# A six-layer network on one core: the experts' transposes a pair further ahead, the zero rows behind the second sample's norm, and a fixed order for the feed-forward's sums

## The chip, the cores and the metric

The kernel runs on one core of one Trainium2 chip. The metric is device time in microseconds (us) of one launch, which computes the whole network for a batch of eight samples. A core has five engines, each with an instruction stream of its own that is executed in order: TensorE (PE in the profile; its weight loads are shown as PEld), VectorE (DVE), ScalarE (ACT), GpSimd (POOL) and SyncE (SP). SyncE issues nearly all transfers; it is written SPq where the profile speaks of its queue. An instruction that waits for a signal of another engine holds everything behind it on its own engine.

## The reference

The input is x of shape (8, 256, 32, 32). Six layers follow one another: an attention with convolutions and a gated convolutional feed-forward, a deformable convolution, a causal attention, a feed-forward on half of the tokens, an attention with squared scores, and a mixture of eight experts. The change touches the last three, where a sample is 1024 tokens of 256 numbers. Cut to these:

```
def _L2_ffn_ref(x, attention_mask, wr, br, w1, b1, w2, b2):
    weights = (jnp.einsum('bsd,do->bso', x, wr) + br)[..., 0]
    _, idx = jax.lax.top_k(weights, k)                 # k = 512 of 1024 tokens
    sel_idx = idx[:, :kk]                              # kk = 511
    sel = jnp.take_along_axis(x, sel_idx[:, :, None], axis=1)
    h = jax.nn.gelu(jnp.einsum('bkd,dh->bkh', sel, w1) + b1)     # 256 -> 1024
    y = jnp.einsum('bkh,hd->bkd', h, w2) + b2                    # 1024 -> 256
    y = y * jnp.take_along_axis(weights, sel_idx, axis=1)[..., None]
    return jnp.zeros_like(x).at[batch_idx, sel_idx].set(y) + x

def _L3_attn_ref(x, qkv_w, qkv_b, proj_w, proj_b):     # 8 heads of 32
    scores = jnp.einsum('bnhd,bmhd->bhnm', q, k) * scale
    t = jnp.square(scores + 5.0)
    attn = t / jnp.sum(t, axis=-1, keepdims=True)
    return jnp.einsum('bhnm,bmhd->bnhd', attn, v).reshape(B, N, D) @ proj_w.T + proj_b

def _moe(tokens, router_w, w1, b1, w2, b2):            # 8 experts, 2 of them for a token
    probs = jax.nn.softmax(tokens @ router_w.T, axis=-1)
    rw, re = jax.lax.top_k(probs, 2)
    rw = rw / jnp.maximum(rw.sum(-1, keepdims=True), 1e-12)
    out = tokens
    for e in range(E):
        h = jax.nn.gelu(tokens @ w1[e] + b1[e], approximate=False)
        out = out + combine[:, e:e + 1] * (h @ w2[e] + b2[e])
    return out
```

Each of these layers is called as `t = t + layer(_ln_t(t))`, with `_ln_t` the normalisation of a token.

## The kernel before

**How work is ordered.** Each layer is a Python generator (`fast0` to `fast3e`) that writes instructions and yields between pieces. A layer's first pieces ("head") are drawn while the layer before it still runs. Inside a layer, `spread` (L1067) lays one generator's pieces evenly beside another's, and `by_time` (L1093) merges several by due times. What the generators write is then put in a final order on each engine by a scheduler; an instruction handed to `net.pinned` (L1042) keeps its written place among the other pinned ones of its engine. `scatter` (L1023) is an indirect transfer from POOL that writes rows to places given by an index; `settled` (L1034) makes a load wait for all the scatters of a group.

**Feed-forward (`fast2f`, about 2640 to 2935 us).** For each sample, `before(b)` norms the tokens and computes a token's score as eight sums on VectorE (L2116, one for each 128 tokens, into a column of `wcol`), then adds the bias `br` (L2119, "wcol"). TensorE transposes `wcol` (L2124, "wrow"), ScalarE copies the rows, and comparisons give each token its rank. `place(b)` scatters tokens in that order to memory, `ready(b)` loads the best 512, transposes them on TensorE (L2178, "xs") and copies them out on VectorE (L2183, "xk"). `main(b)` does the two products: h, gelu, and y with sums over 1024 (L2200); VectorE adds the bias b2 to y in two halves (L2207, "y add"). The streams of several samples are interleaved, so that the scores of one sample lie beside the y products of another on VectorE. Neither L2119 nor L2207 is pinned.

**Attention (`fast3`, about 2935 to 3950 us).** Sample b's attention has 33 steps (`attention`), each with four products s of keys and queries, two squares on ScalarE and four products A with the values; at the end of a chunk VectorE scales the sum (L2660, "o"), and adds the projection (L2666). Beside sample b's steps, `between(b)` is spread: the routing of sample b - 1 (`Routes.route`: norm, store of the normed rows at L2376 "mox", scores of the eight experts, ranks), and the norm and projections of sample b + 1 (`norm`, `projections`). `norm` loads the sample at L2555, writes the normed tokens (`token_norm_steps`, L1019) to a tile `xt`, whose buffer the router's `mo_x` shares, and transposes them on TensorE (L2564, "xn"). For b = 0 there is no sample to route, and `between(0)` begins with `Routes.fill` (L2345): one tile of zeros (a memset at L2350, three small sums at L2352) is stored eight times by SP (L2359, "so<-zero"), to fill the three sorted lists of tokens with rows that no token will take.

**Experts (`fast3e`, about 3950 to 4370 us).** The samples are in three groups (0 to 2, 3 to 5, 6 and 7). `Routes.sort(g)` scatters each group's tokens twice, once for each chosen expert, in the order of experts, into its sorted list in memory ("so"), a token's destination beside it. `experts` then goes over the 76 pairs of blocks of 128 sorted rows, two blocks each but for the last of a group with an odd number. For a pair q:

- `load(q)` loads the rows into `xs` (L2779), one of five buffers, four pairs ahead (`AHEAD`).
- `weights(q)` copies the first product's weights of the blocks' experts on ScalarE (L2792).
- `fetch(q)` transposes the rows on TensorE (L2807, "a") and copies them out on VectorE (L2809, "xk", two buffers).
- `first(q)` does the first product (L2821, "h", sixteen for a pair) and four gelus on ScalarE (L2827, "hid").
- `second(q)` casts the destinations to integers on POOL (L2839, "to"), does the second product (L2843, "y"), adds the bias on VectorE (L2847) and scatters the result (L1026).

`combine(g)` adds up the results of a finished group while the next group runs: loads yg, VectorE sums (L2909, "s"), transposes (L2920, "oT") and stores. The rows of the last group are sorted beside the first groups' pairs; `sorting` is the number of steps over which this is spread. The loop of `experts` is, in the kernel before:

```
            weights(0)
            fetch(0)
            yield
            for q in range(len(pairs)):
                weights(q + 1)
                first(q)
                yield
                fetch(q + 1)
                if q:
                    second(q - 1)
                yield
            second(len(pairs) - 1)
```

Of the kernel before, what the change touches and what calls it, by code (L numbers as in the profile page):

```python
# [10 lines left out]
F32 = mybir.dt.float32  # L11
# [6 lines left out]
P = 128  # L18
B = 8
C = 256  # L20
# [2023 lines left out]
def fast2f(net, io):  # L2044
# [5 lines left out]
    with ExitStack() as ctx, ExitStack() as mid:  # L2050
# [26 lines left out]
        def before(b):  # L2077
# [37 lines left out]
            for t in range(NT):  # L2115
                nc.vector.scalar_tensor_tensor(  # L2116
                    junk[:, :C], xn[:, t, :], 1.0, wr, ALU.mult, ALU.mult, accum_out=wcol[:, t : t + 1]
                )
            nc.vector.tensor_scalar(wcol, wcol, vec[:, 10:11], None, ALU.add)  # L2119
            yield  # L2120
            yield from scaled(s, 2)
            ps = pair("wrow")
# [63 lines left out]
        def main(b):  # L2186
            xk = xks.pop(b)
            hid = own["two"].tile([P, H // P, S], F32, tag="hid", name="hid")
            for m in range(H // P):
                ps = bank("h")  # L2190
                net.linear(ps, w1, xk, bass.ts(m, P), slice(0, S))
                net.pinned(nc.scalar.activation(hid[:, m, :], ps, AF.Gelu_apprx_tanh, bias=vec[:, m : m + 1]))
                yield
            y = own["two"].tile([P, 4, C], F32, tag="y", name="y")
            pk = picked[b] = dr.tile([S, C], F32, tag=f"pk{b}", name=f"pk{b}")
            for t2 in range(0, 4, 2):
                ps = bank("y")
                for i in range(2):
                    for k in range(H // P):
                        made = nc.tensor.matmul(  # L2200
                            ps[:, bass.ts(i, C)], lhsT=hid[:, k, bass.ts(t2 + i, P)], rhs=w2[:, k, :],
                            start=(k == 0), stop=(k == H // P - 1),
                        )
                        if k == 0:
                            net.pinned(made)
                    yield
                nc.vector.tensor_tensor(  # L2207
                    y[:, t2 : t2 + 2], ps.rearrange("p (t c) -> p t c", c=C),
                    b2.unsqueeze(1).to_broadcast([P, 2, C]), ALU.add,
                )  # L2210
            nc.sync.dma_start(out=pk.rearrange("(t p) c -> p t c", p=P), in_=y)
            yield
# [83 lines left out]
class Routes:  # L2296
# [49 lines left out]
    def fill(self):  # L2346

        nc = self.net.nc
        zero = self.rows_of.tile([P, len(GROUPS), ROW], F32, tag="xl", name="zero")
        nc.vector.memset(zero, 0.0)  # L2350
        for g, (lo, hi) in enumerate(GROUPS):
            nc.vector.tensor_scalar(  # L2352
                zero[:, g, C:], self.dest[:, 0:1].to_broadcast([P, ROW - C]), float((hi - lo) * 2 * N), None, ALU.add
            )
        for g, so in enumerate(self.sorteds):
            self.fills[g] = []
            for lo in range(0, TILES[g], 26):
                hi = min(TILES[g], lo + 26)
                ins = nc.sync.dma_start(  # L2359
                    out=so[lo * P : hi * P].rearrange("(t p) c -> p t c", p=P),  # L2360
                    in_=zero[:, g : g + 1].to_broadcast([P, hi - lo, ROW]),
                )
                self.fills[g].append(ins.ins)
                yield

# [140 lines left out]
def fast3(net, io):  # L2506
# [4 lines left out]
    with ExitStack() as ctx, ExitStack() as tok, ExitStack() as att, ExitStack() as bef:  # L2511
# [175 lines left out]
        def between(b):  # L2687

            if b:
                yield from routes.route(b - 1, xs[b - 1], one, pair)  # L2690
            else:
                yield from routes.fill()
            if b + 1 < B:
                yield from norm(b + 1)
                yield from projections(b + 1)
            else:
                yield from net.head()

# [26 lines left out]
def fast3e(net, io):  # L2725
# [4 lines left out]
    with ExitStack() as ctx:  # L2730
# [7 lines left out]
        two = io.pool(ctx, "f3eb", 2)  # L2738
        four = io.pool(ctx, "f3ed", 4)
        five = io.pool(ctx, "f3ec", 5)  # L2740
        psP = io.pool(ctx, "f3ep", 1, PSUM)
        psM = io.pool(ctx, "f3em", 2, PSUM)
        b2 = net.load(one, "f3e_b2")
# [6 lines left out]
        def bank(tag):  # L2750
            return psM.tile([P, 2, C], F32, tag=tag, name=tag)
# [14 lines left out]
            return held[eng, g, i]  # L2766

        def experts():
            xss, xks, w1s, hids = {}, {}, {}, {}

            def load(q):
                if q >= len(pairs):
# [25 lines left out]
            def fetch(q):  # L2798
                if q >= len(pairs):
                    return  # L2800
                g, blocks = pairs[q]
                n = len(blocks)
                load(q + AHEAD)
                xs, ps = xss[q], bank("a")
                for j in range(n):
                    for c in range(KC):
                        nc.tensor.transpose(ps[:, j, bass.ts(c, P)], xs[:, j, bass.ts(c, P)], net.ident)  # L2807
                xks[q] = two.tile([P, 2, KC, P], F32, tag="xk", name="xk")
                nc.vector.tensor_copy(  # L2809
                    xks[q][:, :n].rearrange("p j k n -> p (j k n)"), ps[:, :n].rearrange("p j c -> p (j c)")  # L2810
                )

            def first(q):
                g, blocks = pairs[q]
# [17 lines left out]
            def second(q):  # L2832
                g, blocks = pairs[q]
                n, (lo, hi) = len(blocks), GROUPS[g]
                ps = bank("y")
                y = five.tile([P, 2, C], F32, tag="y", name="y")
                hid, xs = hids.pop(q), xss.pop(q)
                to = five.tile([P, 2], I32, tag="to", name="to")
                net.pinned(nc.gpsimd.tensor_copy(to[:, :n], xs[:, :n, C]))  # L2839
                for j, i in enumerate(blocks):  # L2840
                    w = w2[:, bass.ds(expert(PE, g, i), 1)].rearrange("p e k o -> p (e k) o")
                    for k in range(KC):
                        nc.tensor.matmul(  # L2843
                            ps[:, j, :], lhsT=hid[:, j, k, :], rhs=w[:, k, :], start=(k == 0), stop=(k == KC - 1)
                        )
                for j, i in enumerate(blocks):
                    nc.vector.tensor_tensor(  # L2847
                        y[:, j], ps[:, j], b2[:, bass.ds(expert(DVE, g, i) * C, C)], ALU.add
                    )
                    net.scatter(  # L2850
                        f"f3y_{g}", out=r.results[g], in_=y[:, j], in_offset=None,
                        out_offset=bass.IndirectOffsetOnAxis(ap=to[:, j : j + 1], axis=0),
                        bounds_check=(hi - lo) * 2 * N - 1, oob_is_err=False,
                    )
# [2 lines left out]
                load(q)  # L2857
            weights(0)
            fetch(0)
            yield  # L2860
            for q in range(len(pairs)):
                weights(q + 1)
                first(q)
                yield
                fetch(q + 1)
                if q:
                    second(q - 1)
                yield
# [67 lines left out]

        r.rows_of = side.pool(rest, "mox2", 6)
        sum_pool, y_pool = io.pool(ctx, "f3es", 3), io.pool(ctx, "f3ey", 5)
        sorting = sum(steps[:-1]) - lead - 2 * AHEAD - 2
        streams = [[0, 1, all_pairs], [0.5, sorting / (1 + NT * (GROUPS[-1][1] - GROUPS[-1][0])), r.sort(len(GROUPS) - 1)]]  # L2940
        at = -lead
        for g, (lo, hi) in enumerate(GROUPS[:-1]):
# [278 lines left out]
```

## Time and profile before

| | us |
|---|---|
| Median of three runs (lowest to highest) | 4359.39 (4353.24 to 4366.02) |
| The profiled execution's own time | 4372.2 |
| Its span | 4370.4 |
| PE busy over the span | 4008.9 (92%) |
| DVE busy | 2298.0 (53%) |
| ACT busy | 2228.2 (51%) |
| POOL busy | 564.7 (13%) |
| Idle of PE, 2640 to 2935 (feed-forward) | 37.0 |
| Idle of PE, 2935 to 3950 (attention) | 18.6 |
| Idle of PE, 3950 to 4030 (experts beside the last routing) | 12.6 |
| Idle of PE, 4030 to 4335 (experts) | 35.4 |
| Idle of PE, 4335 to 4371 (last sums) | 24.7 |

Idle is the length of the stretch less PE's busy time in it. A wait in the profile is the idle time of an engine before an instruction, and is put down to the signal that came last: "PE wrow L2124 <- DVE wcol L2119: 17.2, 3, 9.2" means that TensorE's transposes of line 2124 waited for VectorE's instruction of line 2119 for 17.2 us in all, three times, at the longest 9.2. A wait that ends in "issue" is one for which no signal is recorded. The granted clock is the share of full speed that TensorE had. In a timeline of single instructions, times are counted from the start of the span. The trace lacks a few per cent of TensorE's records, so counts there can be a little short.

### The profile page before, as it was taken

Reading aid. Unit: us, or ns where it says so; the run is one execution under the profiler, and the core shown is the slowest. Engines: PE = TensorE matmul, PEld = TensorE weight load, DVE = VectorE, ACT = ScalarE, POOL = GpSimd, SP = SyncE. Lnnn points to the kernel's source line nnn. Section 1 sums busy time; section 2 is a strip of 40 time slices with the busy share of each in tenths; the row PEclk is TensorE's granted clock in tenths of the full one; section 3 lists DMA queues with packets and bytes.
Section 4 is the critical chain, followed back from the end, with each engine's and each line's share of the span. In section 5 each row is a group of like instructions: output and inputs, shape, how many; then the busy total and the mean of one; then the engine's idle time right before and its main releaser. Section 6 shows DMA issues by size and latency. Waiting matters only on the chain. (4 is left out here: it accounts for less than half of the span.)

```text
span 4370.4 us, 53086 instructions
## 1 busy us (share of the span) xinstructions
PE 4008.9 (92%) x20006; PEld 1944.2 (44%) x20006; DVE 2298.0 (53%) x3995; ACT 2228.2 (51%) x2966; POOL 564.7 (13%) x645
## 2 busy tenths in 40 slices
PE   8989999999888889989999988889999999998887
PEld 3223333333333444444444435554444444336776
DVE  2387877887886577752222246642332323324345
ACT  3455555555453366643433454425665556665444
POOL 0000000000000000000000013331000150134653
PEclk9988999999898999999999988899999999999998
DMA  2212222222213111110100012346100040145566
GB/s 89 67 59 84 88 74 89 86 76 80 79 47 116 62 42 58 40 43 1 39 20 20 29 48 93 118 145 186 37 30 30 20 127 30 35 132 179 186 211 212
DMA packets 190636, 350.34 MB, mean 80 GB/s; under 512 B 24121, under 2 KB 134668, under 8 KB 178852
## 3 DMA queue, kind: packets, MB, share of 16 engines
q1 hardware_dynamic: 167124, 294.10, 20.8%
q0 software_dynamic: 19440, 46.45, 3.2%
q10 hardware_dynamic: 3808, 6.29, 0.4%
q8 instruction: 162, 2.65, 0.3%
q14 instruction: 102, 0.84, 0.1%
HBM read 175.15 MB, written 153.89 MB: 75 GB/s over the span
## 5 line engine op out<-in xcount | busy, mean ns | idle before, releaser
L1246 DVE SCALAR_TENSOR_TENSOR a<-hp,w_f_vec,a 128x961 f32<-128x961 f32 (+1 forms) x496 | 608.5, 1232 | 154.3 <-ACT a L1239 146.2
L2677 ACT ACTIVATE e<-s,five 128x1024 f32<-128x1024 f32 x512 | 539.2, 1110 | 276.9 <-PE s L2671 260.6
L2671 PE MATMUL s<-q,k 32*128 32x512 f32 x2048 | 349.2, 645 | 7.9 <-DVE cnt L2437 2.0
L78 PE MATMUL pi<-xn,w_l_wpi 128*128 128x512 f32 x512 | 268.1, 670 | 41.5 <-DVE u L1496 31.0
L1399 ACT ACTIVATE e<-s 128x1024 f32<-128x1024 f32 x256 | 249.3, 1020 | 109.0 <-PE s L1393 106.3
L2655 PE MATMUL A<-e,v 128*32 128x512 f32 x2048 | 279.6, 611 | 0.3 <-ACT e L2677 0.3
L1353 DVE TENSOR_TENSOR sum<-sum,e 128x1024 f32<-128x1024 f32 x192 | 230.7, 1218 | 87.6 <-ACT e L1399 87.5
L1357 PE MATMUL A<-e,va 128*32 128x512 f32 x2048 | 268.8, 606 | 0.0
L1434 ACT ACTIVATE hp<-pi,pib 128x512 f32<-128x512 f32 x128 | 87.6, 688 | 229.5 <-PE pi L78 223.4
L1393 PE MATMUL s<-q,k 32*128 32x512 f32 x1024 | 199.4, 664 | 0.2 <-ACT e L1399 0.2
L2821 PE MATMUL h<-xk,w 128*128 128x128 f32 x1192 | 159.2, 290 | 43.1 <-DVE xk L2809 33.7
L78 PEld LDWEIGHTS pi<-xn,w_l_wpi 128*128 128x128 f32 x512 | 104.6, 214 | 199.0 <-issue 118.7
L2671 PEld LDWEIGHTS s<-q,k 32*128 32x128 f32 x2048 | 111.2, 184 | 173.7 <-issue 99.2
L2821 PEld LDWEIGHTS h<-xk,w 128*128 128x128 f32 x1192 | 153.1, 204 | 54.9 <-DVE xk L2809 38.9
L1721 PE MATMUL pos<-pos,w_f_sel 64*128 64x512 f32 x576 | 163.6, 629 | 9.3 <-ACT ax L1732 2.9
L1026 POOL DMA_INDIRECT res<-y,to x149 | 150.1, 1007 | 153.3 <-issue 135.2
L2792 ACT COPY w<-w_l3f_w 128x512 f32 x149 | 92.6, 625 | 138.3 <-PE h L2821 107.3
L1307 POOL MEMSET thrice<- 32x128 f32 x32 | 6.3, 196 | 1085.0 <-PE pe L1324 1062.3
L2843 PE MATMUL y<-w_l3f_w,hid 128*128 x596 | 143.0, 382 | 0.2 <-ACT hid L2827 0.2
L1026 POOL DMA_INDIRECT so<-xl,rows x128 | 129.6, 1012 | 91.7 <-issue 62.0
L1357 PEld LDWEIGHTS A<-e,va 128*32 128x32 f32 x2048 | 58.8, 110 | 175.6 <-issue 175.6
L2584 DVE COPY v<-v 128x1024 f32<-128x1024 f32 x16 | 19.5, 1223 | 217.0 <-PE v L78 217.0
(404 smaller groups left out, 7149.8 us busy)
## 6 DMA issues: line engine op xcount, KB each, us to landing
x<-d SPq DMA_DIRECT2D x31, 1024.0 KB
xs<-so SPq DMA_DIRECT2D x73, 260.0 KB
so<-zero SPq DMA_DIRECT2D x5, 3380.0 KB
thrice<-v SPq DMA_DIRECT2D x256, 64.0 KB
gated<-st SPq DMA_DIRECT2D x32, 512.0 KB
hc<-gated SPq DMA_DIRECT2D x32, 512.0 KB
d<-x SPq DMA_DIRECT2D x16, 1024.0 KB
xl<-mox SPq DMA_DIRECT2D x64, 256.0 KB
```

Source lines behind the costliest of these rows:

```text
L78: self.nc.tensor.matmul(ps, lhsT=w[:, i, m], rhs=src[:, i, cols], start=(i == 0), stop=(i == k - 1))
L1026: made = self.nc.gpsimd.indirect_dma_start(**args)
L1246: nc.vector.scalar_tensor_tensor(to, fr, taps(t_), to, ALU.mult, ALU.add)
L1353: nc.vector.tensor_tensor(half, half, e[j], ALU.add)
L1357: nc.tensor.matmul(state["A"][32 * h : 32 * h + 32, c, :], lhsT=vas[b][:, kt, c, 32 * h : 32 * h + 32], rhs=e[h // 2][:, h % 2, :], start= ...
L1393: nc.tensor.matmul(ss[h // 2][:, h % 2], lhsT=ks[b][32 * h : 32 * h + 32, bass.ts(kt, P)], rhs=qs[b][32 * h : 32 * h + 32, bass.ts(gq, HF) ...
L1399: nc.scalar.activation(es[i][j], ss[j], AF.Exp, scale=SCALE)
L1721: nc.tensor.matmul(ps[:, bass.ts(h, HF)], lhsT=sel[r, t, xy, :], rhs=poss[b][r, :], start=True, stop=True)
L2655: nc.tensor.matmul(A[32 * h : 32 * h + 32], lhsT=v[:, kt, c * P + 32 * h : c * P + 32 * h + 32], rhs=e[:, h, :], start=first, stop=last,)
L2671: nc.tensor.matmul(ss[h // 2][:, h % 2], lhsT=k[32 * h : 32 * h + 32, c, bass.ts(kt, P)], rhs=q[32 * h : 32 * h + 32, c, bass.ts(hh, HF)], ...
L2677: nc.scalar.activation(e[:, 2 * j : 2 * j + 2], ss[j], AF.Square, scale=SCALE, bias=five)
L2821: nc.tensor.matmul(ps[:, j, m], lhsT=ws[j][:, k, bass.ts(m, P)], rhs=xk[:, j, k], start=(k == 0), stop=(k == KC - 1),)
```

## The change

Three places are edited.

In the feed-forward, the bias add on the scores (L2119) and the bias add on y (L2207) are pinned, so VectorE does them in the order in which the generators write them.

In the attention, `Routes.fill` is drawn behind the norm and the projections of sample 1 rather than ahead of them, and its eight stores are pinned. The pieces of the norm and the projections are so drawn ten steps of the attention earlier (from step 5 of 33, not 15).

In the experts, `fetch` runs two pairs ahead of `first`: pairs 0 and 1 are fetched at the start, and the loop fetches q + 2. The copy xk has three buffers in a pool of its own, the cast "to" moves from `second` to `fetch`, and `sorting` is two steps shorter.

```
@@ fast2f, before(b)
-            nc.vector.tensor_scalar(wcol, wcol, vec[:, 10:11], None, ALU.add)
+            net.pinned(nc.vector.tensor_scalar(wcol, wcol, vec[:, 10:11], None, ALU.add))
@@ fast2f, main(b)
-                nc.vector.tensor_tensor(
-                    y[:, t2 : t2 + 2], ps.rearrange("p (t c) -> p t c", c=C),
-                    b2.unsqueeze(1).to_broadcast([P, 2, C]), ALU.add,
+                net.pinned(
+                    nc.vector.tensor_tensor(
+                        y[:, t2 : t2 + 2], ps.rearrange("p (t c) -> p t c", c=C),
+                        b2.unsqueeze(1).to_broadcast([P, 2, C]), ALU.add,
+                    )
                 )
@@ Routes.fill
                     in_=zero[:, g : g + 1].to_broadcast([P, hi - lo, ROW]),
                 )
+                self.net.pinned(ins)
                 self.fills[g].append(ins.ins)
@@ fast3, between(b)
             if b:
                 yield from routes.route(b - 1, xs[b - 1], one, pair)
-            else:
-                yield from routes.fill()
             if b + 1 < B:
                 yield from norm(b + 1)
                 yield from projections(b + 1)
+                if b == 0:
+                    yield from routes.fill()
@@ fast3e
+        three = io.pool(ctx, "f3ek", 3)
@@ fast3e, fetch(q)
-                xs, ps = xss[q], bank("a")
+                xs, ps = xss.pop(q), bank("a")
...
-                xks[q] = two.tile([P, 2, KC, P], F32, tag="xk", name="xk")
+                xks[q] = three.tile([P, 2, KC, P], F32, tag="xk", name="xk")
...
+                to = tos[q] = five.tile([P, 2], I32, tag="to", name="to")
+                net.pinned(nc.gpsimd.tensor_copy(to[:, :n], xs[:, :n, C]))
@@ fast3e, second(q)
-                hid, xs = hids.pop(q), xss.pop(q)
-                to = five.tile([P, 2], I32, tag="to", name="to")
-                net.pinned(nc.gpsimd.tensor_copy(to[:, :n], xs[:, :n, C]))
+                hid, to = hids.pop(q), tos.pop(q)
@@ fast3e, experts
             weights(0)
             fetch(0)
+            fetch(1)
             yield
             for q in range(len(pairs)):
                 weights(q + 1)
                 first(q)
                 yield
-                fetch(q + 1)
+                fetch(q + 2)
@@ fast3e
-        sorting = sum(steps[:-1]) - lead - 2 * AHEAD - 2
+        sorting = sum(steps[:-1]) - lead - 2 * AHEAD - 4
```

## The prediction

> **What bounds the kernel now.** I read the page's head first, then busy time by stretches cut at the stages, then TensorE's waits in each stretch, then the queue that issues transfers. The head and the stretches:
>
> ```profile
> span 4370.4 us, 53086 instructions
> PE 4008.9 (92%) x20006; PEld 1944.2 (44%) x20006; DVE 2298.0 (53%) x3995; ACT 2228.2 (51%) x2966; POOL 564.7 (13%) x645
> ...
> 2640.00:2935.00 295.00, 257.98 (x962) 177.06 (x960) 171.10 (x643) 130.32 (x204) 107.64 (x111) 0.92 0.34 107
> 2935.00:3950.00 1015.00, 996.37 (x5848) 413.68 (x5848) 315.63 (x875) 612.98 (x613) 186.30 (x176) 0.98 0.24 75
> 3950.00:4030.00 80.00, 67.45 (x434) 60.13 (x433) 41.56 (x132) 40.14 (x92) 30.74 (x37) 0.94 0.55 183
> 4030.00:4335.00 305.00, 269.61 (x1820) 248.84 (x1819) 139.56 (x309) 149.04 (x377) 172.31 (x233) 0.96 0.63 202
> ```
>
> A stretch gives its length, the busy time of PE, PEld, DVE, ACT and POOL, the granted clock, DMA share and GB/s. TensorE is the bound; what can be had is its idle time, and the clock lost behind it, in the feed-forward (295.0 - 258.0 = 37.0 us idle, clock 0.92) and in the experts (35.4 us idle of 305, clock 0.96; 12.6 of the 80 before). The attention between idles 18.6 of 1015. TensorE's waits in the three places, then the transfer queue's in the experts:
>
> ```profile
> PE wrow L2124 <- DVE wcol L2119: 17.2, 3, 9.2
> PE wrow L2124 <- issue: 4.8, 1, 4.8
> PE wrow L2124 <- DVE junk L2116: 3.3, 1, 3.3
> ...
> PE xn L2564 <- DVE xt L1019: 9.0, 1, 9.0
> PE kT L2596 <- DVE v L2584: 2.5, 1, 2.5
> ...
> PE h L2821 <- DVE xk L2809: 7.8, 4, 4.7
> ...
> PE h L2821 <- DVE xk L2809: 25.9, 12, 6.4
> PE h L2821 <- issue: 5.8, 4, 2.6
> PE h L2821 <- DVE bey_o L2972: 2.2, 1, 2.2
> PE h L2821 <- DVE s L2909: 1.3, 1, 1.3
> ...
> SPq L2779 <- POOL to L2839: 17.0, 7, 4.4
> ```
>
> Feed-forward: transposes of the score (wrow) wait for VectorE's wcol. Head of attention: they wait for the first norm. Experts: h, the first product, waits for the copy xk, and only for that.
>
> **Part A, the feed-forward's sums.** No instruction is added. In six of eight samples VectorE's order goes from five score sums, y add, three sums, wcol, to eight sums, wcol, y add; TensorE's order stays (y sums, wrow, xs, last y, h). The y add waits for a signal of TensorE that comes late: in the sample of the 9.2 us wait it starts at 2783.4, though the y products are recorded as done by 2773. Behind that signal stand y 0.69, three sums of 0.53 and wcol 0.23 = 2.5 us, and only then wrow. Nothing covers this: the four gaps at wrow are 17.2 + 4.8 + 3.3 = 25.3 us. After the change wrow needs only ScalarE's rows and the sums. The y add still waits, and the copy xk (1.22) for h is behind it, so a late signal now stops h instead, about 2.2 us of wrow and xs later. If the signal is late whatever is in front of it, four times 2.5 = 10 us go. If it is late because of the stop itself, up to 22 of the 25.3 go. The clock read 0.5 for 6.8, 10.2, 6.8 and 10.2 us behind the four gaps, 34 us in which half, 17, is lost; with all gaps shortened about 13 of it returns. If the lateness is only one of the record, nothing goes. Ends 0 and -35; no row is nearer to one, so I take the middle, **-17**.
>
> **Part B, the zero rows.** The eight stores of zeros (19.6 MB; the memset 0.71 and the three sums 0.31 stay where VectorE has them, at the head) leave the SP queue's place between the loads of samples 1 and 2 for one behind sample 1's projections. The row of those stores:
>
> ```profile
> L2359 SPq DMA_DIRECT2D so<-zero x8: 360/1229/9282, 2933.9 to 2993.2; - x8
> ...
> so<-zero SPq DMA_DIRECT2D x5, 3380.0 KB
> ```
>
> Gained: the load of sample 1's x, issued at 2932.7, landed after 6.9 us with fills beside it, where such a load alone takes 3.9; VectorE takes its statistics ahead of sample 0's norm, and 2.5 of the 9.0 us at xn are that wait. The 2.5 us at kT are gathers (8 x 1.25 us on POOL) that landed late. So 5.0 us at most, nothing at least; -4. The load of sample 2's x, issued at 3001.8 behind the fills, landed after 14.6 us and held VectorE 9.4, but TensorE did not stop: no gain.
>
> Price: the queue is passed in order. All eight now go out back to back at about 3086, when the statistics of sample 1 are stored, and the store of the router's normed rows (mox), the two stores behind it and the next loads follow them. With fills running the page shows 336 to 340 GB/s, so 19.6 MB take 58 us, to 3144, and mox (issued at 3112.8 before, landed after 3.9) lands near 3148. The norm of sample 2 (VectorE, xt, 3148.6 before) writes into the buffer which that store reads; behind it on VectorE stand o (3151.5) and the sum on proj, which the attention's TensorE needs. At the mean 286 GB/s of that stretch (fills and all) the store lands near 3159: VectorE held 10, TensorE 8 with the clock. I take +6 of 0 to +8; Part B is **+2**, ends -5 and +8. The two engines' own order is the same from step 32 of 33 on.
>
> [...]
>
> **Part C, the experts.** Per pair of blocks TensorE has h 1.78, a (xs transposes) 0.44, y 1.73 = 3.95 us, and many pairs take just that. Order before: h(q), a(q+1), y(q-1), h(q+1): the copy xk (0.69) has only y to hide behind, 1.73 - 0.69 = 1.0 us of slack. Whatever delays TensorE's signal or puts s sums (four, 1.91) ahead of xk by more shows as a wait. After: a(q+2), so xk(q+1) has a full pair more, 5 us. The next limit is gelu: h(q) to y(q), 0.44 + 1.73 + 1.78 + 0.44 less 1.14 = 3.2 us. The cast "to" (POOL 0.21, 76 times) is moved, not added, and frees the xs buffer two pairs earlier; the 17.0 us of SP's wait for it go, which TensorE did not feel (xs arrives four pairs ahead). The third xk buffer costs space, no time. The sort of the last group is spread two steps tighter, some 1% more POOL per step.
>
> What is there to gain: the waits at h, 7.8 + 25.9 + 5.8 + 2.2 + 1.3 = 43.0 us in about 22 events, mostly 1 to 2.9, one 6.4; and clock, (1 - 0.96) x 305 + (1 - 0.94) x 80 = 17 us (behind the 6.4 us gap h reads 3.78 for 1.95). All of it: -60. If the late signal holds TensorE itself, only VectorE's share of each event, about 0.75 us, returns: 22 x 0.75 = -16. Both explanations fit the bursts of late signals that I see ahead of the gaps, so the middle: **-38**. The 3.2 us of gelu's slack leave 1.5 and 3.2 of the two longest gaps (4.7 and 6.4), which the middle covers.
>
> [...]
>
> **Sum** against the profiled execution: 4372.2 - 17 + 2 - 38 = 4319. That execution is 12.8 above the median of the runs, 4359.4, and waits of this kind may be a part of those 12.8; a gain of 53 would give 4306, a third of 12.8 off the gain gives **4310**.
>
> **Rivals.** (1) TensorE is held, not signalled late: A -10, B +2, C -16 = -24, 4335. For it: the y add's start 10 us behind the products. Against: a whole pair between h and its copy absorbs also a held engine's tail if the stop was for the copy. (2) Lateness in the record, or hidden anyway: A 0, C -3, B +2: 4358. Against: the granted clock falls behind these gaps, so the idleness is real. (3) The other side, one mechanism: the fills ahead of the mox store. Under 316 GB/s (19.6 MB over 3086 to 3148) VectorE's xt is held, and o with it. At 200, what the experts reach, they take 98 us, to 3184, mox near 3188, VectorE held 39 and TensorE some 37: with A and C at (2), 4359 + 34 = 4393, with them as forecast still 4341. It decides when the drain falls under about 250 GB/s and A and C fail. For it: fills held the queue 9.3 us once. Against: 336 to 340 in the slices with fills. (4) POOL becomes the bound in the experts: 0.21 + 2.0 + 0.3 of scatters and, per 3.2 pairs, 2.84 of sorting = 3.65 us against 3.95 a pair; it caps the gain if its descriptors are slower: C -20, 4328. (5) The edits change no order, because the scheduler had these orders already: the records of before show the old order in each (wcol behind the y add, xk one pair ahead), so no chance of its own.
>
> **How the numbers follow.** Forecast 0.50; (1) 0.20; (2) 0.11; (3) 0.10; (4) 0.09. 0.3% is 13 us, about what a measurement can tell from no change: faster under 4346, slower over 4372. Forecast and (4) are faster, of (1) 0.17, of (3) 0.01: 0.77. (2) and 0.03 of (1): 0.13 with rounding. The rest of (3), 0.10, is slower. Range: the low end is the forecast with four fifths of the strong ends (-35, -5, -60 = -100), 4278; the high end takes in (1) and (2) up to 4358 and leaves out (3) and the strongest tail, 2 in 10.
>
> **What would show it.** In the profile after: A right if the wait of wrow for wcol is gone and what h waits for xk is under 15 us; wrong if it comes back whole at h. B right if xn's wait is near 6.5 and an xt wait on a mox transfer appears near 3150 with TensorE idle under 8. C right if h's waits for xk fall under 8 us and the clock of the experts is 0.99; if they turn into waits of y for hid, the late signal was TensorE's own. POOL idle "issue" time near nothing would be rival (4). A gap of tens of us near 3150 to 3190, or a longer experts' stage, makes the prediction wrong.

## The result, and the profile after

The changed kernel took 4341.37 us in the median of twenty runs (4335.03 to 4357.47), the kernel before 4358.48 in twenty on the same chip (4337.83 to 4376.32). The ratio is 0.9965, with a 95% interval of 0.9953 to 0.9978: 15 us faster (10 to 20), where the prediction had 49 against the median and 53 against the profiled execution. The new profiled execution took 4340.78 us, so it stands at its median, while the one of before stood 12.8 above the first three runs and 13.7 above these twenty: between the two profiles 31 us went, twice what the medians say. About half of that has to be put down to scatter.

The head of the page after, then busy time by stretches, cut at about the same work as before (length, busy time of PE, PEld, DVE, ACT and POOL, granted clock, DMA share, GB/s):

```profile
span 4339.0 us, 53110 instructions
PE 4005.5 (92%) x20006; PEld 1940.8 (45%) x20006; DVE 2294.6 (53%) x3995; ACT 2224.9 (51%) x2966; POOL 564.2 (13%) x645
```

```profile
2636.00:2914.00 278.00, 255.09 (x963) 172.78 (x961) 170.13 (x637) 130.22 (x204) 108.68 (x112) 0.96 0.35 112
2914.00:3941.00 1027.00, 999.30 (x5852) 413.11 (x5852) 318.72 (x885) 612.85 (x613) 185.93 (x176) 0.98 0.24 75
3941.00:4020.00 79.00, 72.27 (x472) 65.71 (x471) 43.26 (x134) 41.81 (x97) 33.73 (x44) 0.94 0.61 202
4020.00:4304.00 284.00, 264.82 (x1779) 245.47 (x1778) 133.19 (x304) 144.52 (x371) 169.37 (x228) 0.96 0.65 212
```

The feed-forward is 17 us shorter than before (278 for 295) and the experts 22 (363 for 385), but the attention between is 12 us longer (1027 for 1015). (Finer marks, in the next section, give 14.5 and 21 us shorter and 9 longer.) TensorE's waits say where. This is the view of waits for TensorE, first the feed-forward, then the first 300 us of attention, then the experts:

```profile
PE y L2200 <- issue: 11.3, 11, 1.8
PE xs L2178 <- issue: 5.0, 4, 1.8
PE wrow L2124 <- issue: 2.0, 4, 1.2
PE wrow L2124 <- DVE wcol L2119: 1.9, 1, 1.9
...
PE s L2674 <- ACT e L2680: 12.6, 2, 11.6
PE xn L2567 <- DVE xt L1019: 9.4, 1, 9.4
...
PE h L2827 <- DVE xk L2813: 9.8, 4, 4.6
PE h L2827 <- issue: 6.2, 12, 1.0
PE y L2847 <- issue: 3.7, 8, 1.0
```

In the feed-forward the waits for the score are gone but for 1.9 us, and in their place TensorE stops up to 1.8 us at a time for nothing that is recorded ("issue"): 18 us in all. In the attention there is a new gap of 11.6 us, and the wait at xn is as long as it was. In the experts, xk is waited for four times, not sixteen.

The new gap begins on another engine. VectorE's waits, near 3120 us and in the experts:

```profile
DVE tn_s L1003 <- DMA x<-d: 15.9, 1, 15.9
...
DVE s L2914 <- DMA yg<-res: 9.8, 2, 6.9
DVE bey_j L2974 <- DMA bey_s<-sums: 7.9, 1, 7.9
```

VectorE stands 15.9 us at the statistics of sample 3, which wait for that sample's load. ScalarE's small steps for sample 2's norm wait for VectorE, the squares stand behind them on ScalarE, and TensorE's next s behind the squares. The clock then reads 0.5 for 20.5 us, from 3129.2 to 3149.6: the last 10 us of the gap and 10.7 us of work behind it. What SP issued there, before and after (start, length of the issues, line, transfer, count):

```profile
3112.80 0.33 SPq L2376 DMA_DIRECT2D mox<-mo_x  x1
3117.43 0.33 SPq L2378 DMA_DIRECT2D mos<-x  x1
3117.86 2.49 SPq L2487 DMA_DIRECT2D xl<-mox  x3
3121.98 0.33 SPq L2555 DMA_DIRECT2D x<-d  x1
```

```profile
3090.20 21.84 SPq L2361 DMA_DIRECT2D so<-zero  x3
3112.15 5.24 SPq L2379 DMA_DIRECT2D mox<-mo_x  x1
3117.48 0.81 SPq L2381 DMA_DIRECT2D mos<-x  x1
3126.87 1.41 SPq L2490 DMA_DIRECT2D xl<-mox  x3
3129.33 0.33 SPq L2558 DMA_DIRECT2D x<-d  x1
```

The clock times look alike, but TensorE was 23 us further in its work after the change than before at this time: the load of sample 3 leaves SP 30 us later in the program. Before, it had some 17 us to spare.

### The profile page after: what moved, and what is told of

The parts are those of the page before. It is cut to its first block, busy times and chain, and to the rows that moved or that the text cites. A ratio compares the mean times of both kernels' runs of the same rounds, so it can differ in the third digit from the quotient of the medians.

```text
span 4339.0 us, 53110 instructions
## 1 busy us (share of the span) xinstructions
PE 4005.5 (92%) x20006; PEld 1940.8 (45%) x20006; DVE 2294.6 (53%) x3995; ACT 2224.9 (51%) x2966; POOL 564.2 (13%) x645
## 5 line engine op out<-in xcount | busy, mean ns | idle before, releaser
L78 PE MATMUL s<-q,k 128*128 128x512 f32 (+3 forms) x384 | 132.5, 488 | 0.0
```

Source lines behind the costliest of these rows:

```text
L78: self.nc.tensor.matmul(ps, lhsT=w[:, i, m], rhs=src[:, i, cols], start=(i == 0), stop=(i == k - 1))
```

## The experiments

The stages of two profiles can be compared more finely than whole runs. I took six marks, each the start of one ScalarE instruction that every trace has: the third sample's scaling in the feed-forward, the first exponential of the attention's norm, the squares number 75, 118 and 495 of the 512 (counted from 0), and the last copy of an expert's weights. "Feed" is from the first to the second, "head" to the third, "next" to the fourth (82 us of sample 1's attention, where the new gap lies), "rest" to the fifth, "experts" to the sixth. All in us, from one profiled execution each:

| kernel | feed | head | next | rest | experts | ratio to before (95% interval) |
|---|---|---|---|---|---|---|
| before | 280.6 | 181.9 | 82.3 | 724.9 | 395.3 | |
| changed | 266.1 | 177.5 | 100.0 | 720.8 | 374.1 | 0.9965 (0.9953 to 0.9978) |
| a_only | 274.5 | 184.2 | 82.5 | 725.9 | 396.6 | 0.9973 (0.9961 to 0.9984) |
| b_only | 271.6 | 180.9 | 100.1 | 727.4 | 403.4 | 1.0004 (0.9988 to 1.0020) |
| c_only | 277.2 | 185.0 | 82.3 | 723.8 | 376.1 | 0.9945 (0.9923 to 0.9967) |
| a_c | 276.5 | 185.8 | 82.3 | 721.6 | 372.4 | 0.9939 (0.9926 to 0.9952) |
| fills_pool_late | 275.2 | 178.9 | 100.7 | 730.6 | 375.1 | 0.9963 (0.9950 to 0.9977) |
| fills_spread | 273.3 | 186.6 | 82.5 | 727.2 | 375.9 | 0.9937 (0.9913 to 0.9962) |
| best3 | 271.3 | 178.8 | 82.5 | 727.8 | 368.4 | 0.9910 (0.9890 to 0.9931) |
| before_again | 239.1 | 185.7 | 82.4 | 720.6 | 366.1 | |
| all_again | 237.0 | 177.5 | 99.4 | 718.1 | 354.0 | 0.9996 (0.9982 to 1.0010) |
| a_c_again | 236.8 | 185.4 | 82.5 | 723.7 | 355.5 | 0.9976 (0.9966 to 0.9986) |
| fills_pool | 235.9 | 177.6 | 82.5 | 718.0 | 360.0 | 0.9970 (0.9958 to 0.9983) |
| flag_early | 238.7 | 185.5 | 82.3 | 717.4 | 343.7 | 0.9960 (0.9944 to 0.9976) |
| best | 238.9 | 177.7 | 82.5 | 718.2 | 343.8 | 0.9938 (0.9922 to 0.9954) |
| ahead3 | 237.4 | 185.2 | 82.5 | 719.5 | 450.2 | 1.0232 (1.0212 to 1.0251) |
| ahead3_to8 | 237.2 | 181.8 | 82.5 | 722.9 | 348.8 | 0.9962 (0.9948 to 0.9975) |
| late_own | 239.1 | 177.7 | 92.7 | 718.6 | 358.0 | 0.9990 (0.9978 to 1.0001) |
| sp_own | 235.6 | 177.8 | 96.6 | 719.0 | 355.3 | 1.0002 (0.9987 to 1.0017) |

The rows fall into two halves. The kernel before took 4358, 4375 and 4372 us in the sets of runs of the upper half, and 4292, 4294 and 4296 in those of the lower half; a set shares one chip. Like kernels differ between the halves in the feed-forward (29 to 42 us) and the experts (17 to 29), and hardly elsewhere.

### The parts one by one: a_only, b_only, c_only, a_c

a_only is the kernel before with the two pins of part A:

```
-            nc.vector.tensor_scalar(wcol, wcol, vec[:, 10:11], None, ALU.add)
+            net.pinned(nc.vector.tensor_scalar(wcol, wcol, vec[:, 10:11], None, ALU.add))
...
-                nc.vector.tensor_tensor(
+                net.pinned(nc.vector.tensor_tensor(
                     y[:, t2 : t2 + 2], ps.rearrange("p (t c) -> p t c", c=C),
```

> Part A alone, on the kernel before. Theory 1 (the parts add up, and what one pair of profiles shows of each is right: A -16, B +14, C -21 us): 16 us faster, ratio 0.996, and in the profile no wait of wrow for wcol over 3 us, while short stalls of TensorE without a recorded signal (1 to 2 us, three or four a sample) remain. Theory 2 (the stage differences between the two profiles are mostly scatter between executions, some 6 us for each part): under 6 us faster, ratio 0.999, and waits of h for xk in place of those of wrow.

It is 12 us faster (7 to 17). The waits of TensorE in its feed-forward:

```profile
PE y L2200 <- issue: 12.4, 10, 1.8
PE xs L2178 <- issue: 10.1, 12, 1.8
PE h L78 <- DVE xk L2183: 3.3, 1, 3.3
```

The waits at wrow, 25.3 us in the profile of before, are gone, but 22.5 us of pauses without a signal stand there, where before had 7.4 at y and 4.8 at wrow. Its feed-forward in the table, 274.5, is not clearly under the others' without part A (280.6, 271.6, 277.2). The mean over the upper half is 272.8 with A (six profiles) and 276.5 without (three): 4 us, and less than the 9 to 10 us by which like profiles differ. The profile that the prediction was read from had the slowest of these feed-forwards, and the longest waits at wrow: 25.3 us, where b_only has 8.3 and c_only 15.4, neither of them with the pins.

b_only is the kernel before with part B:

```
+                self.net.pinned(ins)
...
-            else:
-                yield from routes.fill()
...
+                if b == 0:
+                    yield from routes.fill()
```

> Part B alone. Theory 1: 14 us slower, ratio 1.003: near 3145 us VectorE waits some 16 us for the load of sample 3, which stands behind the fills and the store of the normed rows in the queue; TensorE idles 11 to 12 us and runs at half clock for about 20 us. Theory 2 (the stall belongs to that one execution, or to B together with C's or A's timing): within 5 us of before, and the wait for the load under 5 us. My prediction on record said +2.

The time is within its interval of no change, +2 us (-5 to +9), but the stall is there as in the changed kernel: a wait of 14.9 us for the load, 10.6 us of TensorE, and 100.1 us for 82.3 in "next". The two expectations so came true by halves: the stall of the first, the time of the second.

c_only is the kernel before with all of part C (of its edit, the loop of the experts is shown):

```
             fetch(0)
+            fetch(1)
...
-                fetch(q + 1)
+                fetch(q + 2)
```

> Part C alone. Theory 1: 21 us faster, ratio 0.995; of the 43 us of waits of h some 19 remain, led by waits for xk of 4 to 7 us behind an instruction of VectorE that waits for a transfer (the flag's sums, the first sum of a finished group). Theory 2 (scatter): 6 us or less, ratio 0.9985 or more. The prediction on record said -38, ratio 0.991.

24 us faster (14 to 34), and the experts are 19 to 27 us shorter than in the three traces without C. Its waits at h are 9.2 us for xk and 10.4 of pauses.

a_c is the changed kernel with part B taken back:

```
+            else:
+                yield from routes.fill()
...
-                if b == 0:
-                    yield from routes.fill()
```

> The changed kernel without part B. Theory 1 (parts add): -37 us, ratio 0.9915, and faster than the changed kernel by 14. Theory 2: between -10 and -15, no better than the changed kernel (ratio 0.9965) by more than 4 us.

27 us faster than before (21 to 32). That is 9 less than A and C measured singly add up to, and 12 more than the changed kernel, with part B, gained in its own set.

### The same work without the pauses: all_again, before_again, a_c_again

all_again is the changed kernel and before_again the kernel before, with no edit; a_c_again is a_c.

> The changed kernel itself, unchanged, to stand beside the next three on one chip. The theory now (A -12, B +2 to +14, C -24 from the runs of the parts): ratio 0.9965 as first measured. In the profile, near 3125 us, VectorE waits about 16 us for the load of sample 3 and TensorE idles 11 to 12.

> The kernel before, for a second profile. In the traces so far TensorE pauses without a recorded signal in the feed-forward (23 to 37 us between 2560 and 2900 in the six traces of the first two chips, none in the four of the third) while the order of work is the same. If the pauses belong to the chip, this trace has either some 24 us of them, or none; where there are none, the waits of wrow for wcol are under 6 us and those of h for xk under 25 even before the change.

> The changed kernel without part B once more, beside the next two. On a chip with pauses: ratio 0.994, as measured there. On one without: A has little to move, C still has its short waits: 0.997.

On these chips the change is worth nothing that can be measured: 0.9996, that is -2 us (-8 to +4). Part B's stall is there (99.4), and without B the kernel is 10 us faster than before (6 to 15). The trace of before_again explains it. TensorE's waits in its feed-forward, from the first mark on:

```profile
PE xs L2178 <- DMA xs<-so: 4.4, 3, 3.0
PE wrow L2124 <- DVE wcol L2119: 0.4, 2, 0.2
```

The order of work is the one of before, with y's add in front of wcol, and wrow waits 0.4 us, not 25.3. There are no pauses either, and so no late signal. (The 23 to 37 us that the expectation named include a wait of 11 us at the very head of the stage, which all traces have; the pauses behind it are 12 to 25.) In the experts it waits 18.6 us for xk and the flag, not 43:

```profile
PE h L2821 <- DVE xk L2809: 11.7, 5, 4.7
PE h L2821 <- DVE bey_o L2972: 6.9, 1, 6.9
```

So what A and much of C were to remove looks like the echo of these pauses in other engines' queues. Removing the echo leaves the pauses. No run adds or takes away a pause on one chip, so this rests on the comparison of chips. What makes them was not found: TensorE's own instructions stand ready without a recorded wait, of the stages compared here in the feed-forward and the experts alone, on some chips and not on others. Loading of instructions does not go along with them: each feed-forward, of the changed kernel with pauses and of all_again without, has 15 such transfers of 0.3 to 1.5 us, and nine of the twelve pauses over 0.7 us in the first have none within the 4 us before them.

### Part B's price: fills_pool, fills_pool_late, late_own, sp_own, fills_spread

fills_pool gives the eight stores of the changed kernel to POOL's queue:

```
-                ins = nc.sync.dma_start(
+                ins = nc.gpsimd.dma_start(
                     out=so[lo * P : hi * P].rearrange("(t p) c -> p t c", p=P),
```

> The changed kernel with the eight fills issued by POOL's queue in the same place of the program. If B's stall comes from the order of SP's queue (the store of the normed rows and the load of sample 3 stand behind fills that block the queue), both go out about 20 to 30 us earlier, VectorE's wait for the load falls from 16 to under 3 us, TensorE's 11.6 us gap and the 20 us at half clock go, and the kernel is 10 to 17 us faster than the changed one (ratio 0.992 to 0.994). If the stall comes from the bandwidth that fills take whatever queue issues them, the load lands late all the same: wait still over 10 us, ratio 0.9965.

The stall is gone (82.5), the head is as short as in the changed kernel (177.6), and the kernel is 13 us faster than before, 11 more than all_again in the same set. But it did not test what was meant: POOL had nothing in front of the stores and issued them at 2922 to 2950 us. fills_pool_late holds them back by one small instruction on POOL that needs sample 1's r:

```
         for g, (lo, hi) in enumerate(GROUPS):
...
+        nc.gpsimd.tensor_scalar(zero[:, :, 0:1], late[:, 0, 0:3].unsqueeze(2), 0.0, None, ALU.mult)
...
-                    yield from routes.fill()
+                    yield from routes.fill(rs[1])
```

> As fills_pool, where POOL in fact issued the fills at the head (2922 to 2950 us), since nothing stood before them; here one small POOL instruction that reads sample 1's r and clears zeros again holds them to the moment at which the changed kernel issues them, near 3060. Queue theory (what costs is that SP's queue is held by the fills in front of the store of the normed rows and the load of sample 3): SP issues both as without fills, the stretch from sample 1's first square to 82 us later stays near 82.5 us, not 100, and the time is that of fills_pool. Bandwidth theory (the drain itself delays the store and the load, whatever queue they come from): the load still lands 10 us or more late, and the stretch is 95 us or more.

The stall is back in full, 100.7 us, though SP is not held by any store of zeros. VectorE's wait for the load, and what SP issued:

```profile
DVE tn_s L1003 <- DMA x<-d: 16.7, 1, 16.7
```

```profile
3105.46 0.32 SPq L2380 DMA_DIRECT2D mox<-mo_x  x1
3115.42 1.80 SPq L2491 DMA_DIRECT2D xl<-mox  x2
3117.32 1.29 SPq L2382 DMA_DIRECT2D mos<-x  x1
3142.06 0.36 SPq L2491 DMA_DIRECT2D xl<-mox  x1
3142.52 0.41 SPq L2559 DMA_DIRECT2D x<-d  x1
```

The store of the normed rows, which lands after 3.9 us alone, takes 10 before the load of xl that needs it can go. The third load of xl then waits until 3142: the tile of zeros is one of xl's three buffers. late_own and sp_own give it a buffer of its own, with the fills on POOL's queue at the same time and on SP's as changed:

```
-        zero = self.rows_of.tile([P, len(GROUPS), ROW], F32, tag="xl", name="zero")
+        zero = self.one.tile([P, len(GROUPS), ROW], F32, tag="zero", name="zero")
```

> fills_pool_late with the tile of zeros in a buffer of its own (it shared the three buffers of xl). In fills_pool_late the load of sample 3 left SP at 3142.5, behind a load of xl that waited for the fills to have read the zeros. If that buffer was what held it there, the load leaves 10 to 20 us earlier, and the stretch falls from 100.7 to 83 to 90 us. If the bandwidth of the fills is the cause (the store of the normed rows landed after 10 us, not 4, and each load after it too), it stays at 95 or more.

> The changed kernel with the tile of zeros in a buffer of its own. Here SP itself is held by the fills until 3112 and the first load of xl then waits for the store of the normed rows to land behind them (8.5 us, to 3126.9), so the buffer is free by the time it is asked for: the stretch stays at 97 to 100 us, and the wait for the load at 12 or more. If the shared buffer is the whole cause here too, 83 to 90.

late_own lands between its two expectations, at 92.7; sp_own at 96.6, against 99.4 to 100.1. The buffer is worth 8 us on POOL's queue and 3 on SP's, and is not the whole cause on either. With it out of the way the load waits for the next thing, in late_own for the store that frees its own buffer:

```profile
SPq L2559 <- DMA mos<-x: 21.6, 2, 18.1
```

SP waits 18.1 us for a store of 1 MB that it issued itself while the fills run from POOL's queue: it landed 19.7 us after its issue, 4.5 in the kernel before. Between 3062 and 3100 us the packets of POOL's queue took 70.4% of the 16 DMA engines' time (9.00 MB), those of SP's queue 28.5% (3.83 MB), at 339 GB/s in all.

fills_spread keeps the stores on SP's queue, as a stream of their own:

```
-                if b == 0:
-                    yield from routes.fill()
...
+            if b == 1:
+                beside.append((routes.fill(), 8))
```

> The changed kernel with the fills as a stream of their own beside sample 1's attention and with no other change; in SP's order five of the eight then stand at the head behind the loads of samples 1 and 2, and one before and two behind the store of the normed rows, all three ahead of the load of sample 3. Queue theory: about 6.8 MB, 20 us at 336 GB/s, in front of the load in place of 19.6 MB; it had 17 us to spare, so VectorE's wait for it falls from 13 to 16 us to under 6, and the stretch is 83 to 90 us instead of 100. If any fill near the load costs the same, it stays at 97 or more.

No stall (82.5) with three of the fills in front of the load, and the time of a_c (0.9937 and 0.9939). Its five early fills cost the head what part B had saved there (186.6 for 178). The load left SP at 3135.4, 7 us into "next" (3128.0); before it left at its very beginning, with 17 us to spare. In this order the load also goes out ahead of the three loads of xl, not behind them, so the smaller amount is not the only difference. The price hangs on how much is being written when the router's stores and the load of sample 3 come due: three fills in two pieces fit into that spare time, the whole, which took 63 us to land, does not.

### What remains in the experts: ahead3, ahead3_to8, flag_early, best, best3

ahead3 and ahead3_to8 are a_c with the fetch three pairs ahead; the second has eight buffers for the cast's result.

```
-                fetch(q + 2)
+                fetch(q + 3)
```

```
-                to = tos[q] = five.tile([P, 2], I32, tag="to", name="to")
+                to = tos[q] = eight.tile([P, 2], I32, tag="to", name="to")
```

> The changed kernel without part B, the fetch three pairs ahead instead of two (four xk buffers). Theory D (what waits remain in the experts are VectorE's waits for transfers of 7 to 8 us and TensorE's own pauses without a signal): a third pair covers the transfers, the waits of h for xk fall from 11.6 to under 3 us, the pauses without a signal stay at 8 to 11, and 5 to 9 us go against A and C alone (ratio 0.992). Theory E (the late signal simply needs more lookahead): the pauses without a signal go too, 15 us or more (ratio 0.990 or less). Theory F (the third pair collides with loads that come four pairs ahead): slower.

> Three pairs ahead again, now with eight buffers for the cast's result instead of five. If the 100 us of the first try came from the cast (its buffer is free only when the scatter of five pairs before has landed, and POOL and the loads of xs stand behind it), POOL's wait of the cast for scatters falls from 62 to under 10 us and SP's wait for the cast from 287 to under 30, and the kernel comes to A and C alone or up to 8 us under it (Theory D). If the loads of xs or the sorting are the cause, it stays over 1.01 times before.

ahead3 is 100 us slower than before, in the experts and the sums behind them. The waits of SP's queue and of POOL in ahead3:

```profile
SPq L2782 <- POOL to L2816: 287.5, 62, 8.5
```

```profile
POOL to L2816 <- DMA res<-y,to: 62.4, 24, 6.4
```

The cast of pair q + 3 takes the buffer of pair q - 2, whose scatters were issued only a pair before. POOL waits for it to land with the next scatters queued behind it, and SP's loads of xs wait for the cast. With eight buffers POOL's wait for scatters is gone from its view and the kernel is 16 us faster than before (11 to 22), 6 more than a_c_again, though the two intervals overlap. SP still waits 136 us for the cast, which I had expected under 30, but TensorE's view has no wait for the loads behind it.

flag_early is a_c with the four checks behind the flag (the block "bey") written as a stream beside the experts' pairs, loads first, and their first sums pinned:

```
+        streams.append([40, 6, beyond(net, io.pool(ctx, "bey", 1))])
...
-        if whole:
-            beyond(fast, flag)
```

> The changed kernel without part B, and the sums for the flag at the end (four checks of stored sums) brought forward in the experts' program: their loads are written 20 pairs in, their sums three pairs apart behind it. Nothing of the computation is left out. Theory D: the 4.6 to 6 us gap of TensorE at the flag's wait for its load goes, with its half clock: 5 to 8 us faster than A and C alone (ratio 0.9925). If that gap is not of the flag's load, another wait appears in the same place and nothing goes (ratio 0.994).

best is fills_pool with this edit, best3 is best with the fetch three pairs ahead and eight buffers.

> The changed kernel with the fills on POOL's queue and the flag's sums brought forward. If both gains add (each 4 to 13 us on the third chip against the changed kernel): ratio 0.993 without pauses, 0.990 with them, and 3 to 8 us faster than A and C alone. If POOL's stores of zeros only move the wait elsewhere: no faster than A and C alone.

> The fastest kernel so far (best: fills on POOL's queue, flag's sums early) with the fetch three pairs ahead and eight buffers for the cast. If what three pairs add (6 us against two, on A and C) is the transfers' waits that the early flag takes away too, no gain over best: ratio 0.994. If it is TensorE's waits for other things, 0.9925.

In flag_early the experts fall to 343.7 us, 12 under a_c_again's 355.5. The gap at the flag in a_c_again was 8.4 us, with 3.6 us of work at half clock behind it, 1.8 lost: 10 of the 12. By its times flag_early gains 17 us (10 to 24), 7 more than a_c_again, and these intervals overlap too. The experts' stretch of flag_early behind the last routing:

```profile
3975.00:4240.00 265.00, 260.43 (x1843) 245.60 (x1841) 139.87 (x311) 151.93 (x383) 176.16 (x236) 0.99 0.72 230
```

TensorE is busy 260 of 265 us at clock 0.99. In this stretch, without pauses, little but TensorE's own work is left. best gains 27 us (20 to 33) where the changed kernel gains 2. best3 gains 39 (30 to 48) where the changed kernel gains 15. The two ran on different kinds of chip, so whether the third pair adds to best stays open.

## Why the prediction was wrong

The sign was right. The sum was three times too large. By the table, on chips with pauses, the terms were: A -4 for -17; B +12 (-5 in the head, +17.7 in "next") for +2; C -24 for -38. They add up to -16, against the -15 measured. Without pauses they are A -2, B +10 (-7 and +17), C -9.5, together -1.5, against -2. By whole times the parts add up worse: run singly, on another chip than the changed kernel's, they gave -12, +2 and -24, together -34, each with 5 to 10 us of doubt. The stage table is the better witness of the sizes, but it has one profile for each kernel. Rival (1) forecast 4335 with A -10, B +2, C -16. That this is near the 4341 measured is partly luck: its terms are off by 6, 10 and 8 us, and these errors largely cancel.

**Part A.** The step that failed is "If the signal is late whatever is in front of it, four times 2.5 = 10 us go. If it is late because of the stop itself, up to 22 of the 25.3 go", and the middle of -17 taken between. The first half came closest, and by the stage even it was high: the feed-forward is 4 us shorter, the whole kernel 12 by its times (7 to 17). The signal was late, it seems, because TensorE itself stood still, and the 25.3 us were those of one execution. The clock term was misread as well: of the 34 us at half clock "behind the four gaps", 13 lie in the gaps, which the sum already counts as idle. Work at half clock was 20.9 us, so 10 were lost, not 17. Both signs that were to show A right came (no wait of wrow, nothing at h) with a quarter of its price, so they could not tell the price. That "a late signal now stops h instead" is not so either: h waited 3.3 us once in a_only and not at all in the changed kernel's trace. The stop came back without a name. Rival 1, that TensorE is held, was right here, and I set aside its evidence (the y add starts 10 us behind the products) with an argument on the experts.

**Part B.** What was taken from the queue was right: the fills began at 3061 (the 3086 of the text less the some 22 us that the work had moved by then is 3064), and the store of the normed rows landed behind them at 3126.9, 65 us later, where the text had 62. The wait was put in the wrong place. "The norm of sample 2 (VectorE, xt, 3148.6 before) writes into the buffer which that store reads" comes second; ahead of it on VectorE stand the statistics of sample 3, whose load is behind the store, behind three loads of sample 0's rows for the sorting, and behind the store that frees its buffer. That "the next loads follow them" stood in the text, and was not priced. No run shows the term +6, which was the author's estimate within 0 to +8; the stage table has +17.7 in its place: 11.6 us of idle TensorE, and 5.4 us lost in the 10.7 us of work at clock 0.5. That b_only's time came to the +2 of the text is luck, by the table: both terms of it were off, and b_only's interval (-5 to +9) leaves out the +12 of the stages; why stays open. In the head, "the load of sample 1's x" gained nothing: the load of sample 2's x moved up directly behind it, it landed after 7.2 us in place of 6.9, and xn still waits 9.4. The 5 to 7 us there are the gathers' wait at kT (2.5 to 3.7, gone) and others that I did not trace. The rival on the other side named this queue and this kind of wait; its price of 37 us asked for a drain at 200 GB/s, which did not come (336 was read).

**Part C.** The mechanism was right: xk is off the path but for four waits. The mis-sized term is the middle between -60 and -16. Its far end took all 43.0 us of waits at h, and the 17 us of clock behind them, for one kind. Where 43 us stood at h, 19.7 stand after: 9.9 of TensorE's pauses at h and y, and 9.8 at xk. Of these, 4.6 and 2.7 us are two waits behind VectorE, which is held by transfers (7.9 us at the flag, 6.9 at a group's first sum) for longer than the 5 us of slack that a pair more gives. The clock did not come back: 0.96 and 0.94 both times, with 15 us lost before and 15 after, because clusters of pauses of about 1 us and less are followed by half rate too (3.4 us each at 4061, 4136 and 4157). The longest waits of before and after are not of one kind. These are VectorE's waits in the experts of before:

```profile
DVE xk L2809 <- remote: 13.4, 2, 8.6
DVE bey_j L2969 <- DMA bey_s<-sums: 1.9, 1, 1.9
```

The wait of 6.4 us ended at 4183.9, behind a copy xk that VectorE could start only at 4183.2, 8.6 us idle and with no sender named ("remote"), though its transposes are recorded as done by 4175.7. That is the late signal of the feed-forward again, and it is gone. The 4.6 us after are the flag's, for whose load VectorE waited 1.9 us before and 7.9 after. The 4.7 us wait went to 1.1. Gelu, which the text had as the next limit, holds TensorE for 0.3 us.

**The check marks.** h's waits for xk came to 9.8 us, not under 8, the clock to 0.96, not 0.99, xn's wait to 9.4, not 6.5, and the idle time near 3150 to 11.6, not under 8. POOL was no bound (rival 4): busy 169 of 284 us. The sum there is off too: 0.21 + 2.0 + 0.3 and 2.84 for every 3.2 pairs make 3.4 us a pair, not 3.65.

**The base.** The sum was made against a profile 13 us above its median. I took a third of that off the gain; the feed-forward of that execution alone was 4 us over the mean of its kind, and the first 1700 us, which nothing touches, 8 us over the trace after.

## What to carry to other kernels

A wait that one engine's view names may be the shadow of a pause of the waiting engine itself (25.3 us at wrow in the profile of before, 0.4 in before_again, which has no pauses): before counting it as gain, ask what the signal's sender was waiting for, and compare a trace in which the pause is absent. Where half clock and a gap overlap (13 of 34 us here), count their common time once. A block of stores like this one (336 GB/s for some 60 us) was paid by the load that came due while it drained, from either queue tried here; look for the next load's issue, the stores that free its buffer, and the first instruction on VectorE that needs it, in program order. Deeper lookahead needs every buffer on its way deep enough: five buffers for a cast's small result cost 100 us at three pairs ahead, and eight took it away.

## What the runs showed of the hardware

The same kernel took 4292 to 4296 us in three sets of runs and 4358 to 4375 in three others, and what differs in the traces is TensorE's unnamed pauses in two stages (12 to 25 us of idle time in the feed-forward, and the half clock behind them: 266 to 281 us for 236 to 239). Parts A and C are worth 27 us on the one kind and 10 on the other; with part B's stall, 15 and nothing that can be measured.

A store of 1 MB landed 19.7 us after its issue beside 19.8 MB of stores from another engine's queue (the prediction's 19.6 is 1% low), and after 4.5 us without them.

The clock read 0.5 for 3.4 us behind two gaps of 0.8 and 0.9 us (after, at 4061) and at single gaps of 2.0 to 2.9 us (before, at 4059, 4090, 4206, 4257 and 4274).
